# One PSUM bank moved from scores to transposes, with the value products and the first queries in another order

## The chip, the cores and the metric

The kernel runs on one core of a Trainium2 chip. The metric is the device time of one execution in microseconds, as the median of three timed runs; it is 1917.79 us for the kernel before. Everything is float32. Five engines matter: TensorE (PE, with its weight loads as PEld), VectorE (DVE), ScalarE (ACT), GpSimd (POOL) and the DMA queues issued from SyncE (SP) and from the other engines. The engines run side by side, each through its own instructions in order, and wait for each other through semaphores.

## The reference

The reference is one transformer layer on `x` of 16 batches x 512 tokens x 128 features: attention with relative positions, then a mixture of 16 experts of which each token takes one.

```python
# attention: 16 heads of 8; rel_k, rel_v have 2M + 1 = 257 rows
q, k, v = proj(Wq, bq), proj(Wk, bk), proj(Wv, bv)        # of layernorm(x)
idx = clip(r[None, :] - r[:, None], -M, M) + M            # M = 128
content  = einsum('bhqd,bhkd->bhqk', q, k)
relative = einsum('bhqd,qkd->bhqk', q, rel_k[idx])
w = softmax((content + relative) / sqrt(8))
out = einsum('bhqk,bhkd->bhqd', w, v) + einsum('bhqk,qkd->bhqd', w, rel_v[idx])
x = x + layernorm(out @ Wo.T + bo)
# experts: top 1 of 16 by x2 @ w_router.T, plus a shared one; x2 = layernorm(x)
x = x + layernorm(shared(x2) + expert(sigmoid(logit) * x2))
```

## The kernel before

The kernel has two stages. The attention stage runs over 256 passes, `i` = 0 to 255 (and 24 more in which the last results drain). A pass is one batch `b`, one of four pieces `c` of 32 queries in each 128 tokens, and one of four 128-token blocks `n`, so `k = i % 16` counts the passes of a batch (`c = k // 4`, `n = k % 4`). It handles 32 queries against all 512 keys for 16 heads. The heads go in four groups `g` of four, in the order 0, 2, 1, 3 (`ORDER`); a group's four heads and 32 queries are the 128 rows of a tile of scores, 128 x 512, which fills one bank of PSUM. The expert stage then takes sorted rows of 128 tokens at a time through the experts; the change doesn't touch it.

In the steady state pass `i` does, on PE:

- `scores`: four products `ps<-km,qb` (content) and four times eight 32-row products `ps<-relk,qr` (relative), one bank for each group. The relative products of groups 0 and 2 come first, then those of 1 and 3, over the keys within 128 of a query, which are 160 to 288 columns wide, depending on `c` and `n`.
- `turn`: the exponentials `w` of the pass before (`last = i - 1`), four tiles, each with four 128 x 128 transposes into one bank `pt`.
- `attend`: the value products of the pass five back (`old = i - 5`), `pa<-wT,v` and then `pa<-wT,relv`. In passes with `n` = 1, `join_places` puts eight small products in between for the piece nine passes back.
- at the end of many passes one extra product (`spare`): turned sums at `n` = 0, the output projection at `n` = 1, and at `k` = 6, 7, 14 and 15 the next batch's turned x, queries, keys and values.

DVE takes the row maximum of each score bank (`peak`, written `nmax`), ACT the exponentials with their sums (`exps`). The turned tiles leave PSUM through DVE (`ORDER[0]` and `ORDER[2]`, that is groups 0 and 1) and ACT (groups 2 and 3) as `wT`. DVE scales the value products by the sums (`od`, `oz`) and adds over heads (`oT`).

All these instructions are kept in the order in which the program writes them (class `InOrder`). The order of one pass is written out in the loop at lines 787 to 876. It interleaves: scores; two tiles turned; two peaks with their exponentials; copies of those two tiles; two more peaks and exponentials; value products and what leaves from them; two more tiles turned; the extra product; copies of those two tiles.

PSUM has eight banks: five for scores (`ps_s`), two for transposes (`ps_t`), one for all else (`ps_o`, function `bank`). A pool hands its banks out in turn, and a product into a bank waits until what it held last has been read.

Around the passes: `route` picks the expert of a batch's tokens and scatters their rows to DRAM, in small steps that the loop advances once a pass (lines 860 to 874); the last of these steps are four scatters issued by POOL. `expand` has POOL repeat a piece's queries into `qb` and `qr` for the scores. For `qr` the queries go through DRAM (`qd`, then 16 small DMAs into `qz`). `keys_mixed` and `keys_advance` keep on POOL the keys with end rows added. `load_x` issues four DMAs for a batch, on SP.

Before the loop, for batch 0: x is normalised and turned, then queries, keys and values are formed, one after the other in the one bank of `ps_o`, then POOL expands the first piece.

Of the kernel before, what the change touches and what calls it, by code (L numbers as in the profile page):

```python
# [9 lines left out]
F32 = mybir.dt.float32  # L10
I32 = mybir.dt.int32
AF = mybir.ActivationFunctionType
ALU = mybir.AluOpType
# [4 lines left out]
P = 128  # L18
# [32 lines left out]
def relative_attention_then_moe(  # L51
# [42 lines left out]
    with ExitStack() as actx:  # L94
# [2 lines left out]
        bp = actx.enter_context(tc.tile_pool(name="attn_batch", bufs=2))  # L97
        up = actx.enter_context(tc.tile_pool(name="attn_unit", bufs=2))
        sp = actx.enter_context(tc.tile_pool(name="attn_small", bufs=4))
        ps_s = actx.enter_context(tc.tile_pool(name="ps_s", bufs=5, space=PSUM))  # L100
        ps_t = actx.enter_context(tc.tile_pool(name="ps_t", bufs=2, space=PSUM))
        ps_o = actx.enter_context(tc.tile_pool(name="ps_o", bufs=1, space=PSUM))
        pe, act, dve, sp_q, pool = (InOrder(tc, e) for e in (nc.tensor, nc.scalar, nc.vector, nc.sync, nc.gpsimd))

# [7 lines left out]
                )  # L112

        load_x(0)


        wq = wp.tile([P, D], F32, name="wq")
# [26 lines left out]
        for i in range(2):  # L144
            sp_q.dma_start(
                kend[:, i : i + 1], bass.AP(rel_kT.tensor, rel_kT.offset + i * (NR - 1), [[0, H], [NR, HD], [1, 1]])
            )
        act.mul(bq_c, bq_c, qscale)
        bk_hi = wp.tile([P, 1], F32, name="bk_hi")
        relk = wp.tile([P, 504], F32, name="relk")  # L150
# [62 lines left out]
            )  # L213
        msum = wp.tile([P, HG, HD], F32, name="msum")

        batch, wts = {}, {}

        riders = []

        def bank(shape, name):  # L220
            return ps_o.tile(shape, F32, tag="o", name=name)
# [32 lines left out]
        def queries(b):  # L254


            xT = batch[b]["xT"]
            pq = bank([P, S], f"pq{b}")
            pe.matmul(
                pq.rearrange("p (c n q) -> p c n q", n=NKT, c=NC), wq,  # L260
                xT.rearrange("p (n c q) -> p c n q", n=NKT, c=NC), start=True, stop=True,
            )
            qp = bp.tile([P, TQ, S // TQ], F32, tag="qp", name=f"qp{b}")
            qz = bp.tile([P, 8, S // TQ], F32, tag="qz", name=f"qz{b}")
            batch[b].update(qp=qp, qz=qz)

            def leave():
                act.activation(
                    qp.rearrange("p q t -> p t q"), pq.rearrange("p (t q) -> p t q", q=TQ),
                    AF.Identity, bias=bq_c, scale=qscale,  # L270
                )
                qd = dp.tile([P, TQ, S // TQ], F32, tag="qd", name=f"qd{b}", bufs=2)
                sp_q.dma_start(qd, qp)
                batch[b]["qd"] = qd
                if b > 0:
                    queries_turned(b)

            return leave

        def queries_turned(b):  # L280
            qz, qd = batch[b]["qz"], batch[b]["qd"]
            for e in range(2):
                for i in range(TQ):
                    r = e * 64 + (7 - i) * HD
                    queue = act if b == 0 and i % 2 else sp_q
                    queue.dma_start(
                        qz[r : r + HD], qd[e * 64 : (e + 1) * 64, i, :].rearrange("(h d) t -> d h t", d=HD)
                    )

        def keys(b):  # L290

            pk = bank([P, S], f"pk{b}")
# [12 lines left out]

            return leave
# [47 lines left out]

            return leave

        def expand(b, c):

            bt = batch[b]
            tt = slice(c * 16, (c + 1) * 16)  # L360
            qb = up.tile([P, 16, HH, TQ], F32, tag="qb", name=f"qb{b}_{c}")
            pool.tensor_mul(
                qb,
                bt["qp"][:, :, tt].rearrange("p q t -> p t q").unsqueeze(2).to_broadcast([P, 16, HH, TQ]),
                mh4.unsqueeze(1).unsqueeze(3).to_broadcast([P, 16, HH, TQ]),
            )
            qr = up.tile([P, 16, 8, TQ], F32, tag="qr", name=f"qr{b}_{c}")
            pool.tensor_mul(
                qr,
                bt["qz"][:, :, tt].rearrange("p h t -> p t h").unsqueeze(3).to_broadcast([P, 16, 8, TQ]),  # L370
                mq.unsqueeze(1).unsqueeze(1).to_broadcast([P, 16, 8, TQ]),
            )
            batch[b, c] = (qb, qr)

        ORDER = (0, 2, 1, 3)

# [96 lines left out]
        def attend(b, c, n, done=None):  # L473


            wT = wts[b, c][0]
            v = batch[b]["v"]
            Rh = batch[b, c, "R"][0]
            if n == 0:
                batch[b, c, "oT"] = up.tile([P, NKT * 4, TQ], F32, tag="oT", name=f"oT{b}_{c}")  # L480
            oT = batch[b, c, "oT"]
            every3 = bank([P, 3, P], f"pa{b}_{c}_{n}")
            pa = every3[:, 0]
            for kt in range(NKT):
                vn = 1 if kt <= n - 2 else 2 if kt >= n + 2 else 0
                for g in range(HG):
                    r = slice(g * 32, (g + 1) * 32)
                    pe.matmul(
                        pa[r, :], v[:, vn, kt, r], wT[:, n, g, (kt - n) % NKT, :],
                        start=(kt == 0), stop=(kt == NKT - 1),  # L490
                    )
            t = slice(n * 4, n * 4 + 4)
            summed = lambda: None
            if done is not None:
                summed = join_places(every3[:, 1], *done)
            elif riders:
                summed = riders.pop()(every3[:, 1])
            near_done = attend_near(every3[:, 2], b, c, n)

            def leave():  # L500
                od = up.tile([P, 4, HH, TQ], F32, tag="od", name=f"od{b}_{c}_{n}")
                dve.tensor_mul(od, pa.rearrange("p (t h q) -> p t h q", h=HH, q=TQ), Rh[:, t])
                near_done()
                summed()
                dve.tensor_reduce(oT[:, t], od.rearrange("p t h q -> p t q h"), AX.X, ALU.add)

            return leave

        def attend_near(pn, b, c, n):

# [262 lines left out]
        dve.tensor_reduce(mz, mz4.rearrange("p g q -> p q g"), AX.X, ALU.add)  # L773
        dve.tensor_reduce(msum, mj.rearrange("p j g d -> p g d j"), AX.X, ALU.add)
        dve.tensor_add(bk_hi, bk_c, kend[:, 1:2])
        for f in (x_turn, queries, keys):
            f(0)()
        queries_turned(0)
        values(0)()
        expand(0, 0)  # L780
        for n in range(1, NKT):
            keys_mixed(0, n)
        if B > 1:
            load_x(1)
        later_loads()
        routes = {}
        for i in range(total + 24):
# [283 lines left out]
```

## Time and profile before

| | |
|---|---|
| median of 3 runs | 1917.79 us (1917.73 to 1917.93) |
| the profiled execution's own time | 1931.33 us |
| its span, first to last instruction | 1929.6 us |
| busy share of ACT | 63% |
| busy share of POOL | 51% |
| granted TensorE clock, mean | 0.988 |
| first scores begin | 23.44 us |
| scores of the last pass begin | 1650.68 us |

The times of the prediction are made on the profiled execution, which took 13.5 us longer than the median. A profile line has the start and length in us, the engine, the line of the program (nearly all stand under line 47, the helper that keeps the order), the operation, output<-inputs by the program's names, shapes, and the count of merged instructions; in brackets the idle time before it and what ended it. A group in the page's list has its count, total and mean time, and then the engine's idle time before it.

### The profile page before, as it was taken

The page shows a single profiled execution, that of the slowest core. Times are in us where ns is not written, and L with a number is a line of the kernel's source. Part 1 is how long each engine was busy: PE and PEld are TensorE (multiplying, and loading weights), DVE is VectorE, ACT ScalarE, POOL GpSimd, SP SyncE. Part 2 cuts the span into 40 slices and gives each one's busy share as a digit, 9 for nine tenths or more (in the row PEclk, how much of TensorE's full clock was granted, in tenths as well). Part 3 has the DMA queues.
Part 4 walks back from the last instruction along what each step waited for, and adds up shares of the span by engine and source line. Part 5 has one row for each costly group of instructions (what it writes and reads, how often), then busy time and mean ns, then how long its engine had stood idle before and what let it go on. Part 6 is the DMA issues. An engine that isn't in the chain of part 4 may idle for free. (4 is left out here: it accounts for less than half of the span.)

```text
span 1929.6 us, 88255 instructions
## 1 busy us (share of the span) xinstructions
PE 1863.7 (97%) x38268; PEld 1383.0 (72%) x38268; DVE 1528.7 (79%) x4009; ACT 1207.7 (63%) x3077; POOL 989.8 (51%) x1389
## 2 busy tenths in 40 slices
PE   6999999999999999999999999999999999779997
PEld 3667776776777777676767676776767776579997
DVE  4777787878788878788888888787878787757776
ACT  3666666666666666666666666666666665257775
POOL 4345455546455554546454555454645545236666
PEclk9999999999999999999999999999999999879999
DMA  2321100000000000000000000000000000066662
GB/s 77 65 35 40 17 23 5 15 14 5 24 5 24 4 24 3 25 3 25 3 24 5 24 4 16 12 13 16 5 18 5 18 3 9 9 176 180 183 182 87
DMA packets 88328, 68.64 MB, mean 36 GB/s; under 512 B 26440, under 2 KB 74341, under 8 KB 87809
## 3 DMA queue, kind: packets, MB, share of 16 engines
q1 hardware_dynamic: 81248, 53.60, 10.3%
q0 software_dynamic: 4384, 8.57, 1.4%
q8 instruction: 301, 4.93, 1.0%
q10 hardware_dynamic: 2304, 0.80, 0.2%
q14 instruction: 91, 0.74, 0.1%
HBM read 44.79 MB, written 18.75 MB: 33 GB/s over the span
## 5 line engine op out<-in xcount | busy, mean ns | idle before, releaser
L47 ACT ACTIVATE w<-ps,nmax 128x512 f32<-128x512 f32 x1024 | 699.0, 693 | 554.4 <-DVE nmax L47 554.0
L47 DVE TENSOR_REDUCE nmax<-ps 128x1 f32<-128x512 f32 x1024 | 655.1, 681 | 226.4 <-PE ps L47 225.2
L47 PE MATMUL pt<-ident,w 128*128 128x128 f32 x4096 | 562.0, 280 | 4.4 <-DVE wT L47 3.8
L47 PEld LDWEIGHTS pt<-ident,w 128*128 128x128 f32 x4096 | 439.7, 141 | 125.6 <-issue 85.7
L47 DVE COPY wT<-pt 128x512 f32<-128x512 f32 x512 | 348.3, 680 | 1.1 <-PE pt L47 0.7
L47 ACT COPY wT<-pt 128x512 f32<-128x512 f32 x512 | 300.9, 588 | 28.5 <-PE pt L47 26.5
L47 PE MATMUL ps<-km,qb 32*128 32x512 f32 x2048 | 298.4, 647 | 3.5 <-POOL qb L47 3.5
L47 PEld LDWEIGHTS ps<-relk,qr 64*32 64x32 f32 x8192 | 124.4, 106 | 227.6 <-issue 183.9
L47 PE MATMUL pa<-wT,v 128*32 128x128 f32 x8192 | 276.7, 276 | 2.5 <-DVE oz L47 1.4
L47 PE MATMUL ps<-relk,qr 64*32 64x288 f32 (+4 forms) x8192 | 275.5, 378 | 0.0
L47 PEld LDWEIGHTS pa<-wT,v 128*32 128x32 f32 x8192 | 208.1, 109 | 45.2 <-issue 36.0
L47 ACT ACTIVATION_READ_ACCUMULATOR w<-ps,nmax 128x1 f32 x1024 | 211.8, 207 | 0.0
L47 PE MATMUL pa<-wT,relv 128*32 128x48 f32 (+1 forms) x12288 | 199.3, 211 | 6.2 <-issue 5.4
L47 POOL TENSOR_TENSOR Rh<-R,mh 128x512 f32<-128x512 f32 x64 | 66.6, 1040 | 261.0 <-ACT R L47 253.8
L47 PEld LDWEIGHTS pa<-wT,relv 128*32 128x32 f32 x12288 | 186.8, 110 | 11.1 <-issue 11.1
L47 POOL TENSOR_TENSOR qr<-qz,mq 128x1024 f32<-128x1024 f32 x64 | 137.3, 2146 | 0.0
L47 PEld LDWEIGHTS ps<-km,qb 32*128 32x128 f32 x2048 | 82.4, 184 | 59.9 <-issue 32.0
L47 POOL TENSOR_SCALAR km<-kT,kend 128x32 f32<-128x32 f32 (+2 forms) x223 | 115.6, 520 | 1.7 <-PE ps L47 0.9
L47 POOL COPY km<-kT 128x32 f32<-128x32 f32 (+3 forms) x207 | 53.0, 261 | 113.8 <-ACT kT L47 113.8
L47 POOL DMA_INDIRECT out_dram<-f,to x73 | 75.9, 1039 | 46.8 <-issue 26.9
L47 DVE TENSOR_TENSOR od<-pa,Rh 128x128 f32<-128x128 f32 x256 | 72.9, 285 | 32.6 <-PE pa L47 29.7
L47 POOL COPY rb<-rt 128x512 f32<-128x512 f32 x64 | 39.2, 612 | 112.3 <-DVE rt L47 112.1
(168 smaller groups left out, 2331.0 us busy)
## 6 DMA issues: line engine op xcount, KB each, us to landing
gu<-_L_ffn_gate_up_proj_dram SPq DMA_DIRECT2D x73, 256.0 KB
dn<-in_L_ffn_down_proj_dram SPq DMA_DIRECT2D x73, 128.0 KB
rows<-zero SPq DMA_DIRECT2D x19, 266.0 KB
xc<-rows SPq DMA_DIRECT2D x8, 532.0 KB
x_sb<-in_L_attn_x_dram SPq DMA_DIRECT2D x64, 64.0 KB
qd<-qp SPq DMA_DIRECT2D x16, 256.0 KB
qz<-qd SPq DMA_DIRECT2D x248, 16.0 KB
relv<-vext SPq DMA_DIRECT2D x1, 1536.0 KB
```

The lines of the kernel that those rows point to most:

```text
L47: return lambda *a, **k: self.tc.keep_in_program_order(op(*a, **k))
```

## The change

It alters the order of a pass, the banks, the start, and where scatters stand.

The pass: the value products are issued straight behind the scores. The four peaks follow each other on DVE. All four tiles are turned in one stretch behind the value products: three, then on DVE `od`, `oz` and the copy of the first tile, then the fourth. `attend` hands out its DVE work in two parts, by `yield`. ACT copies both its tiles at the end of the pass.

```diff
-        ps_s = actx.enter_context(tc.tile_pool(name="ps_s", bufs=5, space=PSUM))
-        ps_t = actx.enter_context(tc.tile_pool(name="ps_t", bufs=2, space=PSUM))
+        ps_s = actx.enter_context(tc.tile_pool(name="ps_s", bufs=4, space=PSUM))
+        ps_t = actx.enter_context(tc.tile_pool(name="ps_t", bufs=3, space=PSUM))
...
                 dve.tensor_mul(od, pa.rearrange("p (t h q) -> p t h q", h=HH, q=TQ), Rh[:, t])
                 near_done()
+                yield
                 summed()
                 dve.tensor_reduce(oT[:, t], od.rearrange("p t h q -> p t q h"), AX.X, ALU.add)
-
-            return leave
+                yield
+
+            return leave()
...
             if live:
                 scores(b, c, n)
-            if last is not None:
-                T = {g: turn(*at(last), g) for g in ORDER[:2]}
+            leave_a = iter((None, None))
+            if old is not None:
+                leave_a = attend(*at(old), done=done)
+            elif done is not None:
+                join_places(bank([P, P], f"pj{b}"), *done)()
             if live:
-                for g in ORDER[:2]:
+                for g in ORDER:
                     peak(b, c, n, g)
                     exps(b, c, n, g)
             if last is not None:
+                T = {g: turn(*at(last), g) for g in ORDER[:3]}
+            next(leave_a)
+            if last is not None:
                 dve.tensor_copy(*T[ORDER[0]])
-                act.copy(*T[ORDER[1]])
-            if live:
-                for g in ORDER[2:]:
-                    peak(b, c, n, g)
-                    exps(b, c, n, g)
-            if old is not None:
-                attend(*at(old), done=done)()
-            elif done is not None:
-                join_places(bank([P, P], f"pj{b}"), *done)()
-            if last is not None:
-                T = {g: turn(*at(last), g) for g in ORDER[2:]}
+                T[ORDER[3]] = turn(*at(last), ORDER[3])
+            next(leave_a)
             if spare is not None:
                 leave = spare()
             if last is not None:
+                act.copy(*T[ORDER[1]])
                 dve.tensor_copy(*T[ORDER[2]])
                 act.copy(*T[ORDER[3]])
```

The start: 40 transposes of the identity run on PE while x is loaded (`warm`). A matrix `sel` is made on POOL. Batch 0's keys get a bank of `ps_s`. The first 16 of 64 query groups leave PSUM first, PE repeats them by eight products with `sel`, and DVE expands the first piece from there. The other queries go through DRAM as before, now all on SP. Values of batch 0 become the extra product of pass 2, and batch 1's x is loaded ahead of `kext` and `relk`.

```diff
+        def warm(n):
+
+            idle = ps_t.tile([P, NKT, P], F32, tag="t", name="idle")
+            for t in range(n):
+                pe.transpose(idle[:, t % NKT, :], ident, ident)
+
+        warm(40)
...
+        if B > 1:
+            load_x(1)
...
+        sel = up.tile([P, 8 * P], F32, tag="wT", name="sel")
+        nc.gpsimd.memset(sel, 0.0)
+        for h in range(8):
+            nc.gpsimd.affine_select(
+                sel[:, h * P : (h + 1) * P].rearrange("p (e j d) -> p e j d", e=2, j=TQ),
+                sel[:, h * P : (h + 1) * P].rearrange("p (e j d) -> p e j d", e=2, j=TQ),
+                [[-64, 2], [0, TQ], [-1, HD]], ALU.not_equal, 1.0, base=-h * HD, channel_multiplier=1,
+            )
...
+        def repeat_queries(rep_q):
+
+            for h in range(8):
+                pe.matmul(
+                    rep_q[h // 4][:, h % 4].rearrange("p t q -> p q t"), sel[:, h * P : (h + 1) * P],
+                    batch[0]["qp"][:, :, 0:16], start=True, stop=True,
+                )
+
+        def expand_first(rep_q):
+            qb = up.tile([P, 16, HH, TQ], F32, tag="qb", name="qb0_0")
+            qr = up.tile([P, 16, 8, TQ], F32, tag="qr", name="qr0_0")
+            batch[0, 0] = (qb, qr)
+            dve.tensor_mul(
+                qb,
+                batch[0]["qp"][:, :, 0:16].rearrange("p q t -> p t q").unsqueeze(2).to_broadcast([P, 16, HH, TQ]),
+                mh4.unsqueeze(1).unsqueeze(3).to_broadcast([P, 16, HH, TQ]),
+            )
+            for i in range(2):
+                dve.tensor_mul(
+                    qr[:, :, i * 4 : (i + 1) * 4, :].rearrange("p t h q -> p h t q"), rep_q[i],
+                    mq.unsqueeze(1).unsqueeze(1).to_broadcast([P, 4, 16, TQ]),
+                )
...
-        for f in (x_turn, queries, keys):
-            f(0)()
-        queries_turned(0)
-        values(0)()
-        expand(0, 0)
+        x_turn(0)()
+        rep_q = [ps_t.tile([P, 4, 16, TQ], F32, tag="t", name=f"rep_q{i}") for i in range(2)]
+        leave_q = queries(0)
+        leave_k = keys(0)
+        leave_q(0, 16)
+        repeat_queries(rep_q)
+        leave_k()
+        expand_first(rep_q)
+        leave_q(16, S // TQ)()
         for n in range(1, NKT):
             keys_mixed(0, n)
-        if B > 1:
-            load_x(1)
         later_loads()
...
+            if i == 2:
+                spare = lambda: values(0)
```

The scatters: for all but the last three batches the last steps of `route` are taken in passes with `n` = 0, right behind the sums' `rb` on POOL.

```diff
             if n == 0 and 0 <= i - 4 < total:
                 sums(*at(i - 4)[:2])
+                for r in sorted(routes):
+                    if r[0] < B - 3 and i - (r[0] + 1) * 16 - 6 >= 18:
+                        if next(routes[r], StopIteration) is StopIteration:
+                            del routes[r]
                 spare = lambda: sums_turn(*at(i - 4)[:2])
...
-                if r[0] < B - 2:
+                if r[0] < B - 3:
+                    turns = i - (r[0] + 1) * 16 - 6 in (0, 1, 2, 3, 4, 5, 6, 7, 12, 13, 14, 15)
+                elif r[0] < B - 2:
                     turns = i - (r[0] + 1) * 16 - 6 in (0, 1, 2, 3, 4, 5, 6, 7, 12, 13, 14, 15, 16, 17, 19, 20, 21)
```

More of the change, by code (lines that the diff above doesn't have):

```diff
@@ L265, in queries, with leave, turned @@
             batch[b].update(qp=qp, qz=qz)
-            def leave():
+            qd = dp.tile([P, TQ, S // TQ], F32, tag="qd", name=f"qd{b}", bufs=2)
+            def leave(t0=0, t1=S // TQ):
                 act.activation(
-                    qp.rearrange("p q t -> p t q"), pq.rearrange("p (t q) -> p t q", q=TQ),
+                    qp[:, :, t0:t1].rearrange("p q t -> p t q"),
+                    pq[:, t0 * TQ : t1 * TQ].rearrange("p (t q) -> p t q", q=TQ),
                     AF.Identity, bias=bq_c, scale=qscale,
                 )
-                qd = dp.tile([P, TQ, S // TQ], F32, tag="qd", name=f"qd{b}", bufs=2)
-                sp_q.dma_start(qd, qp)
-                batch[b]["qd"] = qd
+                if b == 0 and t0 == 0:
+                    return
+                sp_q.dma_start(qd[:, :, t0:t1], qp[:, :, t0:t1])
+                def turned():
+                    for e in range(2):
+                        for i in range(TQ):
+                            r = e * 64 + (7 - i) * HD
+                            sp_q.dma_start(
+                                qz[r : r + HD, :, t0:t1],
+                                qd[e * 64 : (e + 1) * 64, i, t0:t1].rearrange("(h d) t -> d h t", d=HD),
+                            )
                 if b > 0:
-                    queries_turned(b)
-            return leave
[L280 to L288, printed above, removed]
+                    turned()
+                return turned
+            return leave
         def keys(b):
-            pk = bank([P, S], f"pk{b}")
+            pk = bank([P, S], f"pk{b}") if b > 0 else ps_s.tile([P, S], F32, tag="s", name="pk0")
             pe.matmul(pk, wk, batch[b]["xT"], start=True, stop=True)
@@ L355, in values, with expand @@
             return leave
-        def expand(b, c):
+        def expand(b, c, eng=pool, parts=((0, 16),)):
             bt = batch[b]
-            tt = slice(c * 16, (c + 1) * 16)
             qb = up.tile([P, 16, HH, TQ], F32, tag="qb", name=f"qb{b}_{c}")
-            pool.tensor_mul(
+            qr = up.tile([P, 16, 8, TQ], F32, tag="qr", name=f"qr{b}_{c}")
+            batch[b, c] = (qb, qr)
+            for t0, t1 in parts:
+                n, tt = t1 - t0, slice(c * 16 + t0, c * 16 + t1)
+                eng.tensor_mul(
+                    qb[:, t0:t1],
+                    bt["qp"][:, :, tt].rearrange("p q t -> p t q").unsqueeze(2).to_broadcast([P, n, HH, TQ]),
+                    mh4.unsqueeze(1).unsqueeze(3).to_broadcast([P, n, HH, TQ]),
+                )
+                eng.tensor_mul(
+                    qr[:, t0:t1],
+                    bt["qz"][:, :, tt].rearrange("p h t -> p t h").unsqueeze(3).to_broadcast([P, n, 8, TQ]),
+                    mq.unsqueeze(1).unsqueeze(1).to_broadcast([P, n, 8, TQ]),
+                )
@@ new lines, in repeat_queries @@
+        def repeat_queries(rep_q):
[3 more added lines that the diff above has]
+                    batch[0]["qp"][:, :, 0:16], start=True, stop=True,
+                )
+        def expand_first(rep_q):
[3 more added lines that the diff above has]
+            dve.tensor_mul(
@@ L363, in expand @@
                 qb,
-                bt["qp"][:, :, tt].rearrange("p q t -> p t q").unsqueeze(2).to_broadcast([P, 16, HH, TQ]),
+                batch[0]["qp"][:, :, 0:16].rearrange("p q t -> p t q").unsqueeze(2).to_broadcast([P, 16, HH, TQ]),
                 mh4.unsqueeze(1).unsqueeze(3).to_broadcast([P, 16, HH, TQ]),
             )
[L367 to L372, printed above, removed]
@@ L373, in expand @@
-            batch[b, c] = (qb, qr)
+            for i in range(2):
+                dve.tensor_mul(
+                    qr[:, :, i * 4 : (i + 1) * 4, :].rearrange("p t h q -> p h t q"), rep_q[i],
+                    mq.unsqueeze(1).unsqueeze(1).to_broadcast([P, 4, 16, TQ]),
+                )
         ORDER = (0, 2, 1, 3)
```

## The prediction

> **What bounds the kernel now.** I read the page's busy shares first, then the timeline of one plain pass, then the places where TensorE does wait, then the start. The chain of waits is no help: it holds only the last microsecond. The page:
>
> ```profile
> PE 1863.7 (97%) x38268; PEld 1383.0 (72%) x38268; DVE 1528.7 (79%) x4009; ACT 1207.7 (63%) x3077; POOL 989.8 (51%) x1389
> ...
> L47 POOL TENSOR_TENSOR Rh<-R,mh 128x512 f32<-128x512 f32 x64 | 66.6, 1040 | 261.0 <-ACT R L47 253.8
> ```
>
> PE is busy 97% of the span. DVE at 79% looks like spare room, but shares don't say where in a pass it lies. POOL idles 253.8 us ahead of `Rh`. Now the timeline of a plain pass (batch 0, k = 10; start, length, engine, operation, output<-inputs):
>
> ```profile
> 84.25 1.14 PE L47 MATMUL ps<-km,qb 32*128 32x512 f32 x8
> ...
> 85.32 1.20 PE L47 MATMUL ps<-relk,qr 64*32 64x288 f32 x32
> ...
> 86.20 1.29 DVE L47 TENSOR_REDUCE nmax<-ps 128x1 f32<-128x512 f32 x2 [1.00 <-PE ps L47]
> ...
> 86.45 1.09 PE L47 MATMUL pt<-ident,w 128*128 128x128 f32 x8
> ...
> 87.40 0.68 DVE L47 COPY wT<-pt 128x512 f32<-128x512 f32 x1
> ...
> 87.48 1.08 PE L47 MATMUL pa<-wT,v 128*32 128x128 f32 x32
> ...
> 88.00 1.28 DVE L47 TENSOR_REDUCE nmax<-ps 128x1 f32<-128x512 f32 x2
> ...
> 88.38 0.75 PE L47 MATMUL pa<-wT,relv 128*32 128x64 f32 x48
> ...
> 89.05 1.09 PE L47 MATMUL pt<-ident,w 128*128 128x128 f32 x8
> ...
> 89.89 0.29 DVE L47 TENSOR_TENSOR od<-pa,Rh 128x128 f32<-128x128 f32 x1 [0.61 <-PE pt L47]
> ...
> 90.08 1.14 PE L47 MATMUL ps<-km,qb 32*128 32x512 f32 x8
> 90.10 0.28 DVE L47 TENSOR_TENSOR oz<-pa,Rz 128x128 f32<-128x128 f32 x1
> ...
> 90.30 0.37 DVE L47 TENSOR_REDUCE oT<-od 128x32 f32<-128x128 f32 x1
> 90.58 0.68 DVE L47 COPY wT<-pt 128x512 f32<-128x512 f32 x1
> ```
>
> A pass runs from one `ps<-km` to the next: 84.25 to 90.08, 5.83 us, with no hole on PE. Its six PE stretches are 1.07 (km), 1.13 (relk), 1.02 (two tiles turned), 0.90 (v), 0.68 (relv) and 1.02 (two tiles turned). DVE's first peak comes 1.95 after the pass begins, because it needs the first half of the relk products; then DVE work follows at 0.60 a step (86.20, 87.40, 88.00), so the copies hide in PE's time. Transposes alone show what happens when they don't hide (batch 0's third pass, no value products to cover):
>
> ```profile
> 39.87 0.68 DVE L47 COPY wT<-pt 128x512 f32<-128x512 f32 x1
> ...
> 40.61 0.42 PEld L47 LDWEIGHTS pt<-ident,w 128*128 128x128 f32 x4 [0.83 <-DVE wT L47]
> ```
>
> The copy ends at 39.87 + 0.68 = 40.55, and the tile waiting for that bank starts at 40.61: 0.06 after it. The start:
>
> ```profile
> 7.53 1.08 POOL L47 TENSOR_TENSOR lx_rs<-lx_ve,mhalf 128x4 f32<-128x4 f32 x1 [1.77 <-DVE lx_ve L47]
> ...
> 9.04 1.24 PE L47 MATMUL ptx<-ident,xn 128*128 128x128 f32 x4 [9.04 <-DVE xn L47]
> ...
> 23.34 2.12 POOL L47 TENSOR_TENSOR qr<-qz,mq 128x1024 f32<-128x1024 f32 x1
> ...
> 23.44 1.24 PE L47 MATMUL ps<-km,qb 32*128 32x512 f32 x4 [3.54 <-POOL qb L47]
> ```
>
> The first scores wait until 23.44 for POOL's `qb`. In the timeline the sixth pass (i = 5) starts at 52.78.
>
> **The gain: one switch.** The timeline, instruction by instruction, has transposes 0.109 apart. From the last transpose to the first of v it is 0.203, and the first transpose of a stretch is 0.055 slow. One stretch of four tiles is 1.02 + 8 x 0.109 = 1.90 where two take 2.05. So 0.15 a pass, and a plain pass would be 5.67, if nothing waited. I take it that relk straight into v drains as relk into transposes does, since every switch in this trace starts 0.07 before the modelled end of what ran before.
>
> **The price: a wait.** The fourth tile's bank is the first tile's. In the built program its first transpose waits for DVE's copy of that tile, and DVE now does, in order: four peaks, `od`, `oz`, then that copy. From the pass's start, plain wide pass:
> - first peak 1.95 (86.20 - 84.25)
> - four peaks until `od` is issued, 4 x 0.60 = 2.40
> - `od` and `oz`, 0.21 + 0.20 (89.89, 90.10, 90.30) = 0.41: the copy starts at 4.76
> - copy 0.68 and 0.06 to PE: the fourth tile starts at 5.50
> - its four transposes to the last start, 0.055 + 3 x 0.109 = 0.38, and the drain to the next pass 0.20: 6.08
>
> PE would be ready for that tile at 1.07 + 1.13 + 0.90 + 0.68 + (0.055 + 12 x 0.109) = 5.14. It waits 0.36, and the pass takes 6.08 against 5.83. Queued behind that wait are the pass's extra product and the next scores, hence the next peaks: a closed loop, and no later slack gives it back. Every pass then lasts F + 4.13, F being the first peak's start. F by the width of relk (160, 192, 224, 256, 288 columns) is 1.66, 1.72, 1.77, 1.82, 1.88, each the last less 0.053, half the width's PE time; 0.07 more where n is 2 or 3, since peaks there wait on two semaphores (1.88 in the pass at 77.40, 1.95 in the one at 84.25). Narrow passes lose more: PE gets through relk faster, DVE through four peaks no faster.
>
> An extra product behind the fourth tile costs what it does now (rows' spacing): turned sums or x 0.44, output 0.52, queries 0.88, keys 0.86, values 0.97, route's 0.28 to 0.44. In passes with n = 1 `join_places` (0.22 on PE) now falls into the wait: 6.53 against 6.67. Per pass of a batch, k = 0 to 15, before (starts of km in the timeline; these repeat from batch to batch within some hundredths):
> 6.13 6.67 6.22 5.71 6.10 6.67 6.26 6.49 6.05 7.12 6.43 6.17 6.16 6.67 6.69 6.42, sum 101.96
> after, F + 4.13 + the extra (k = 9 with its 0.45 hole inside the relv products kept):
> 6.23 6.53 6.47 6.02 6.28 6.53 6.51 6.85 6.34 6.98 6.51 6.20 6.39 6.53 6.94 6.83, sum 104.14
> So +2.18 a batch: 14 x 2.18 = 30.5, about 1.5 for batch 0 from its sixth pass (the same lists, k = 5 to 15) and 2 taken for the last batch, whose route differs: +34 us.
>
> **The start.** Removed from the chain: the values' product and its sums, POOL's `qb` and `qr`, and the round trip of queries through DRAM for the first scores. Added: eight products with `sel` (16 PE instructions at 0.109 = 1.75), three DVE products (0.60 to 0.69), and on POOL, ahead of `lx_rs`, a memset of 1024 columns (0.20 for 128, 0.11 for 16: 0.9) and eight selects (0.26 to 0.43, 0.40 taken: 3.2). POOL's setup ended at 5.76, so `lx_rs` moves from 7.53 to about 9.9, and the first transpose from 9.04 to 11.4. Then turn and copy x 1.3, queries 1.1, the first 128 columns out 0.6, pk 0.4 still ahead of them, `sel` products 1.75: scores at 16.5. Pass 1 has no spare bank and begins when the first exponential frees one (1.66 + 0.79 + 0.69 on: 19.7); its banks come 0.67 apart, so its relk starts at 22.75, its first peak at 23.5, its copy 2.40 later, and it ends 0.74 + 0.38 + 0.20 after that, at 27.2 (36.72 before). Passes 2 to 4, F + 3.72 without `od` and `oz`, with values and sums turned as extras, take 6.64, 5.61 and 5.88 and end at 45.3 (52.78 before): -7.5 us. If PE runs at half pace, as it did until 36.2 (transposes 0.213 apart), some 4 us of PE work there doubles: -3.5. If selects are as short as the shortest, -9.5. I take -7.5, since 40 transposes at 0.213 fill 8.5 us before.
>
> Trainium skill, "TensorE: Matmul & The Clock Gate", Part 1: the clock rises after one busy window of about 3.4 us and falls after an idle one. Here the granted clock fell to 0.50 for 97.6 to 101.0 after a window in which PE was busy for 1.46 of 3.40 us, so a whole idle window was not needed. By the page the 1 to 3 us between the last warming transpose and the first real one would cost nothing (-7.5); by the row it may (-3.5).
>
> **Moved at no cost.** The scatters (64 on the page of DMA issues, 1.07 on POOL in the timeline) go behind `rb` in passes with n = 0. The cover is POOL's wait for `R`, 253.8 / 62 = 4.1 us each; without it `od` is late by 1.07, and with it PE. x for batch 1 goes ahead of `kext` on SP: four issues, 1.74 to 2.99 in all, move `kext` from 7.72 to about 8.2 and `relk` by as much, and it is needed at 17.5. Now all 16 `qz` go on SP (5.50 at 77.05), ahead of `vext` and `relv`: `relv` is issued some 4 us later than 26.52, and is needed behind 45. Four score banks instead of five: the last exponential ends at F + 0.79 + 4 x 0.67 = 5.42, the next scores come at 6.08. Cover 0.66; gone, it would add one for one.
>
> Trainium skill, "TensorEngine Tiling (Array Packing)", PSUM Bottleneck: packing speeds up the products, not the copies out of PSUM, which can become the bound. It speaks against this change; the rows say how much, the page doesn't.
>
> **Sum.** +34 - 7.5 = +26.5 on the profiled execution's 1931.33 us (span 1929.6), so 1957.8; on the median of 1917.79, 1944.
>
> **Rivals.**
> - The copy is early enough and only the switch counts: -251 x 0.15 - 7.5 = -45, 1872. For it: the PE rows alone. Against: DVE would have to be at the copy 0.36 sooner in wide passes, 0.58 in narrow ones, and five instructions stand ahead of it, back to back. It pays from a wait under 0.10. 6%.
> - Peaks come late. In the pass after k = 3 the first peak stood at 2.00 instead of 1.72, after k = 9 at 2.24 instead of 1.95, behind route's small DVE operations; before, that cost nothing. In the loop it costs its full size: 3 or 4 passes of 0.3, 1 a batch, +16, 1960. Against: passes grow by 0.1 to 0.4, which lets DVE catch up. 15%.
> - The start gives nothing (POOL's selects, slow PE): 1951. 12%.
> - The wait is there but about 0.11 smaller per pass all through, and start and loop cancel: 1918. Nothing in the rows halves it. 4%.
> - The wait as worked out: 1944, 63%.
>
> For the range I go from 1930 (each pass 0.05 shorter, 12 us) to 1962 (late peaks); outside lie the first rival, the fourth, and a little above. A measurement here can tell about 0.2% from no change. Faster 7%, same 3%, slower 90%.
>
> **What would show it.** In the changed kernel's plain pass: no hole from relk to the third tile; a hole of 0.3 to 0.6 ahead of the fourth, released by DVE `wT`; km to km about 6.08; passes with n = 1 shorter, at 6.53; DVE's peaks four in a row; first scores near 16.5. I am wrong if transposes run sixteen in a row without a hole, or if the waits on PE name ACT's exponentials.

## The result and the profile after

The changed kernel takes 1949.88 us (median of 4 runs, 1947.97 to 1952.67), beside 1917.76 (1917.53 to 1917.93) for the kernel before: ratio 1.0168, 95% interval 1.0156 to 1.0180, so 32 us slower. The forecast was 1944, with a range from 1930 to 1962.

First the page of after: busy shares, then the groups that matter (count, total and mean time, then the engine's idle time before the group and what ended it).

```profile
PE 1843.9 (95%) x38324; PEld 1383.0 (71%) x38324; DVE 1517.3 (78%) x4012; ACT 1217.9 (63%) x3078; POOL 990.0 (51%) x1396
...
L47 PE MATMUL pt<-ident,w 128*128 128x128 f32 x4096 | 554.8, 280 | 57.0 <-DVE wT L47 53.8
L47 PEld LDWEIGHTS pt<-ident,w 128*128 128x128 f32 x4096 | 438.8, 141 | 130.7 <-DVE wT L47 103.0
...
L47 PE MATMUL ps<-km,qb 32*128 32x512 f32 x2048 | 294.8, 641 | 1.5 <-ACT w L47 1.5
...
L47 POOL TENSOR_TENSOR Rh<-R,mh 128x512 f32<-128x512 f32 x64 | 66.3, 1035 | 227.8 <-ACT R L47 221.7
```

TensorE's share fell from 97% to 95% although it does 56 instructions more: it now waits. The transposes have 57.0 us of idle time in front of them, ended by DVE `wT`. The scores wait 1.5 us for exponentials, so four score banks don't bind here. POOL still idles over 220 us ahead of `Rh`. The table of waits (engine and tile, what it waited for: us in total, times, longest) puts the same wait at 53.8 us for TensorE's products and at 103.0 for their weight loads:

```profile
PEld pt L47 <- DVE wT L47: 103.0, 194, 2.6
...
PE pt L47 <- DVE wT L47: 53.8, 164, 2.4
```

Neither is the loss itself, since matmul ends are modelled and overlap the hole; its size comes from starts. The plain pass, batch 0, k = 10, as before (start, length, engine, operation):

```profile
79.20 1.14 PE L47 MATMUL ps<-km,qb 32*128 32x512 f32 x8
...
80.28 1.20 PE L47 MATMUL ps<-relk,qr 64*32 64x288 f32 x32
...
81.15 2.49 DVE L47 TENSOR_REDUCE nmax<-ps 128x1 f32<-128x512 f32 x4 [1.00 <-PE ps L47]
...
81.41 1.08 PE L47 MATMUL pa<-wT,v 128*32 128x128 f32 x32
...
82.30 0.75 PE L47 MATMUL pa<-wT,relv 128*32 128x64 f32 x48
...
82.98 1.53 PE L47 MATMUL pt<-ident,w 128*128 128x128 f32 x12
...
83.55 0.28 DVE L47 TENSOR_TENSOR od<-pa,Rh 128x128 f32<-128x128 f32 x1
83.75 0.28 DVE L47 TENSOR_TENSOR oz<-pa,Rz 128x128 f32<-128x128 f32 x1
...
83.95 0.68 DVE L47 COPY wT<-pt 128x512 f32<-128x512 f32 x1
...
84.69 0.66 PE L47 MATMUL pt<-ident,w 128*128 128x128 f32 x4 [0.17 <-DVE wT L47]
...
85.27 1.14 PE L47 MATMUL ps<-km,qb 32*128 32x512 f32 x8
```

Read it against the prediction's steps. The pass begins at 79.20. The first peak stands at 81.15, 1.95 later; four peaks run in a row as one group of 2.49. Then `od` 83.55, `oz` 83.75, and only at 83.95 the copy of the first tile, 4.75 behind the pass's start (4.76 forecast). The first three tiles run from 82.98 as 12 transposes. The other four start at 84.69, 0.06 behind the copy's end (84.63); without the wait they would follow 0.109 behind the twelfth, at 84.35, so the hole is 0.34. The next pass begins at 85.27: 6.07 us (6.08 forecast) against 5.83.

The start:

```profile
1.71 7.17 PE L47 MATMUL idle<-ident 128*128 128x128 f32 x40 [1.71 <-POOL ident masks.py:199]
...
4.26 2.89 POOL L230 TENSOR_SCALAR_AFFINE_SELECT sel<-sel 128x128 f32<-128x128 f32 x8
...
9.45 1.05 POOL L47 TENSOR_TENSOR lx_rs<-lx_ve,mhalf 128x4 f32<-128x4 f32 x1
...
10.94 1.10 PE L47 MATMUL ptx<-ident,xn 128*128 128x128 f32 x4 [2.06 <-DVE xn L47]
...
16.45 1.14 PE L47 MATMUL ps<-km,qb 32*128 32x512 f32 x8
```

The warming transposes end at 8.88, the selector's eight selects take 0.36 each (0.40 forecast), `lx_rs` stands at 9.45 (9.9 forecast) and the first scores at 16.45 (16.5 forecast, 23.44 before).

The length of a pass, from one `ps<-km` to the next, by k (median over batches). "Before" is the forecast's list, from the first profile; "again" is the kernel before profiled once more (before_again, see below); "copy" is copy_first and "n1" the second run of copy_first_n1 (copy_first_n1_b), two of the experiments:

```
k              0    1    2    3    4    5    6    7    8    9   10   11   12   13   14   15   sum
before       6.13 6.67 6.22 5.71 6.10 6.67 6.26 6.49 6.05 7.12 6.43 6.17 6.16 6.67 6.69 6.42 101.96
again        6.13 6.67 6.22 5.71 6.11 6.67 6.26 6.49 6.05 6.67 6.43 5.90 6.15 6.67 6.68 6.42 101.23
forecast     6.23 6.53 6.47 6.02 6.28 6.53 6.51 6.85 6.34 6.98 6.51 6.20 6.39 6.53 6.94 6.83 104.14
after        6.22 6.47 6.46 6.01 6.27 6.47 6.51 7.17 6.33 6.47 6.80 6.01 6.38 6.47 6.86 6.75 103.65
copy         6.13 6.67 6.20 6.03 6.03 6.67 6.24 6.45 6.05 6.67 6.42 5.96 6.15 6.67 6.67 6.35 101.36
n1           6.13 6.47 6.20 6.03 6.03 6.53 6.24 6.45 6.05 6.47 6.42 5.97 6.16 6.47 6.67 6.35 100.64
```

### The profile page after: what moved, and what is told of

It is laid out like the page before. It is cut to its first block, busy times and chain, and to the rows that moved or that the text cites. A ratio compares the mean times of both kernels' runs of the same rounds, so it can differ in the third digit from the quotient of the medians.

```text
span 1946.1 us, 88498 instructions
## 1 busy us (share of the span) xinstructions
PE 1843.9 (95%) x38324; PEld 1383.0 (71%) x38324; DVE 1517.3 (78%) x4012; ACT 1217.9 (63%) x3078; POOL 990.0 (51%) x1396
## 5 line engine op out<-in xcount | busy, mean ns | idle before, releaser
L47 ACT ACTIVATE w<-ps,nmax 128x512 f32<-128x512 f32 x1024 | 689.7, 686 | 534.9 <-DVE nmax L47 534.8
L47 DVE TENSOR_REDUCE nmax<-ps 128x1 f32<-128x512 f32 x1024 | 635.9, 684 | 274.4 <-PE ps L47 271.7
L47 PE MATMUL pt<-ident,w 128*128 128x128 f32 x4096 | 554.8, 280 | 57.0 <-DVE wT L47 53.8
L47 PEld LDWEIGHTS pt<-ident,w 128*128 128x128 f32 x4096 | 438.8, 141 | 130.7 <-DVE wT L47 103.0
L47 ACT ACTIVATION_READ_ACCUMULATOR w<-ps,nmax 128x1 f32 x1024 | 207.3, 202 | 0.0
L47 PE MATMUL pa<-wT,relv 128*32 128x48 f32 (+1 forms) x12288 | 192.0, 211 | 0.0
L47 POOL DMA_INDIRECT out_dram<-f,to x73 | 75.9, 1039 | 46.8 <-issue 27.5
L47 DVE TENSOR_REDUCE oT<-od 128x32 f32<-128x128 f32 x256 | 95.3, 372 | 0.0
```

The source lines that it names most:

```text
L47: return lambda *a, **k: self.tc.keep_in_program_order(op(*a, **k))
```

## The experiments

Ratios are to the kernel before, run beside each. It stood at 1919.45 us beside order_only, reduce_ahead, copy_first and start_only; at 1921.54 beside before_again, scatter_only, banks_only and two_orders; at 1935.05 beside copy_first_n1 and copy_first_sel; and at 1920.10 beside copy_first_n1_b and n1_old_scatters. So times are compared within a set, and across sets by ratios.

**The new order alone** (`order_only`): before, with the pass's new order and banks; the start and the scatters as they were.

```diff
-ps_s bufs=5, ps_t bufs=2
+ps_s bufs=4, ps_t bufs=3
...
+the loop of a pass and attend()'s two yields, as in the change
```

> Before with the new order of a pass and its banks alone; the start and the scatters as they were. If the fourth tile's wait is the whole cost: the loop's +34 us by the prediction (1952), +38 us by the times (after is 32 above before, and the start's gain is 5.7 in the traces), so 1950 to 1958. If the moved scatters or the start bring part of the loss: clearly less, 1920 to 1945. Plain wide pass 6.07 us in both cases.

Measured: 1960.03 us, ratio 1.0208 (1.0194 to 1.0223), +40.6. The plain pass is 6.07, and weight loads wait 102.2 us for DVE `wT` (103.0 in after). The pass lengths are those of after but for two: pass 7 takes 6.82 (7.17 in after) and pass 9, in which a scatter stands here, 6.65 (6.47). So the loss lies in the order. That it is 2 us above the range has a plain place: passes 11 and 12 of batch 0 took 11.0 and 10.3 us, in after 7.4 and 6.4. These two differ by some us from run to run in every kernel here.

**The dose, upwards** (`reduce_ahead`): after, with the sum into `oT` (and `oj`) also put ahead of the copy.

```diff
             next(leave_a)
+            next(leave_a)
             if last is not None:
                 dve.tensor_copy(*T[ORDER[0]])
                 T[ORDER[3]] = turn(*at(last), ORDER[3])
-            next(leave_a)
```

> After, with VectorE's sum into oT, and in passes with n = 1 the copy oj, moved ahead of the copy of the first turned tile: the opposite of the run before. If the wait sets the pass: +0.28 us in each of 256 passes and +0.2 in 64, so +84 us, 2030 (2015 to 2045). If it doesn't: 1945 to 1955.

Measured: 2040.66 us, ratio 1.0630 (1.0614 to 1.0645). Against after's ratio this is 0.0462 x 1919.45 = +89 us. The plain pass takes 6.35, after's 6.07 plus 0.28; passes with n = 1, where the copy `oj` comes on top, take 7.01, plus 0.54. TensorE's idle time ahead of the transposes, in the page's group:

```profile
L47 PE MATMUL pt<-ident,w 128*128 128x128 f32 x4096 | 561.0, 280 | 141.8 <-DVE wT L47 101.6
```

DVE's instructions ahead of that copy thus cost one for one: the 0.28 of the sum on DVE became 0.28 or 0.29 on 11 of the 16 kinds of pass. Pass 11 grew by 0.51; why is open.

**The dose, downwards** (`copy_first`): after, with the copy ahead of `od` and `oz`.

```diff
-            next(leave_a)
             if last is not None:
                 dve.tensor_copy(*T[ORDER[0]])
                 T[ORDER[3]] = turn(*at(last), ORDER[3])
             next(leave_a)
+            next(leave_a)
```

> After, with VectorE's copy of the first turned tile moved ahead of od and oz (0.21 + 0.20 us). If the fourth tile waits for that copy: the plain wide pass falls from 6.07 to 5.67 (TensorE's own path and the wait are then about equal, F + 3.72 = 5.67), narrow ones by 0.41, sum 256 x 0.39 = 100 us, so 1850 us, below both kernels. If the loss came from four score banks or from the exponentials, nothing changes: 1945 to 1952. If another wait stands right behind this one (late peaks, the output bank that od and oz now free later): 1870 to 1930.

Measured: 1916.47 us, ratio 0.9980 (0.9971 to 0.9989). The sign is right and the loss is gone, but only some 36 us of the 100 came (0.0188 x 1919.45, from the two ratios), as the third case had it. The plain pass shows the first reason:

```profile
81.06 1.14 PE L47 MATMUL ps<-km,qb 32*128 32x512 f32 x8
...
83.01 2.48 DVE L47 TENSOR_REDUCE nmax<-ps 128x1 f32<-128x512 f32 x4 [1.00 <-PE ps L47]
...
84.84 2.09 PE L47 MATMUL pt<-ident,w 128*128 128x128 f32 x16
...
85.53 0.69 DVE L47 COPY wT<-pt 128x512 f32<-128x512 f32 x1
...
86.14 0.28 DVE L47 TENSOR_TENSOR od<-pa,Rh 128x128 f32<-128x128 f32 x1
...
86.34 0.28 DVE L47 TENSOR_TENSOR oz<-pa,Rz 128x128 f32<-128x128 f32 x1
...
86.86 0.31 PEld L47 LDWEIGHTS ps<-km,qb 32*128 32x128 f32 x8 [0.17 <-issue]
```

The four tiles now run as one group of 16. The copy starts at 85.53, not behind the fourth peak at 85.41 (81.06 + 1.95 + 2.40): it now waits for its own tile, whose last transpose ends at 85.49. It ends at 86.22, the fourth tile starts 0.06 later, and the free slot would have been 0.07 sooner. With the slow first transpose behind a hole (0.055) the pass takes 5.80, not 5.67. The second reason stands in the passes with n = 1, where `od`, `oz` and the copy `oj` now end later and the output's product waits for them:

```profile
PEld py L47 <- DVE oj L47: 11.4, 63, 0.7
```

(us in total, times: 0.18 each.) These passes take 6.67, in after 6.47. The output bank, freed by `od`, `oz` and `oj`, is the next thing to end last. And pass 3 gains nothing (6.03): its first peak is late, 2.20 behind the pass's start, behind route's DVE work. Pass 0 gains 0.09 only: its turned sums wait for POOL's `rb` (4.9 us, 15 times).

**copy_first without its new wait** (`copy_first_n1`, and once more as `copy_first_n1_b`):

```diff
+            if done is not None:
+                next(leave_a)
             if last is not None:
                 dve.tensor_copy(*T[ORDER[0]])
                 T[ORDER[3]] = turn(*at(last), ORDER[3])
+            if done is None:
+                next(leave_a)
             next(leave_a)
```

> copy_first, except in passes that join places (n = 1): there od and oz stay ahead of the copy, as in after. If those passes are long in copy_first (6.67 us, in after 6.47) because the output's product waits for the bank that od, oz and oj free: 62 x 0.2 = 12 us less than copy_first, 1904 to 1907 beside a before of 1920; all other passes as in copy_first. If the time is paid back in the passes behind them: 1917.

Measured: 1931.00 us, beside 1935.05 of before; ratio 0.9980 (0.9971 to 0.9988), no better than copy_first. The passes with n = 1 did fall to 6.47, none behind them paid it back, but those with k = 4, 8 and 12 had grown to 6.95, 6.50 and 6.61. The timeline of one with k = 4, batch 3:

```profile
348.94 0.52 PEld L47 LDWEIGHTS pa<-wT,relv 128*32 128x32 f32 x31
349.05 0.94 PE L47 MATMUL pa<-wT,relv 128*32 128x64 f32 x36
349.12 1.12 POOL L47 DMA_INDIRECT rows<-pay,at_i  x1 [0.17 <-issue]
...
349.68 0.17 PEld L47 LDWEIGHTS pa<-wT,relv 128*32 128x32 f32 x5 [0.23 <-issue]
...
350.40 0.26 PEld L47 LDWEIGHTS pa<-wT,relv 128*32 128x32 f32 x12 [0.56 <-issue]
350.42 0.38 PE L47 MATMUL pa<-wT,relv 128*32 128x48 f32 x12 [0.44 <-issue]
...
350.73 2.09 PE L47 MATMUL pt<-ident,w 128*128 128x128 f32 x16
```

A scatter starts on POOL at 349.12. Behind it TensorE's weight loads run dry twice, for 0.23 and 0.56, in the middle of the relv products, waiting for nothing that the profile shows ("issue"). The same kernel was therefore run once more.

> copy_first_n1 once more, unchanged. Its first run had holes inside the value products of passes k = 4, 8 and 12, 1.3 to 1.5 us behind each scatter's start (0.91 + 0.45 + 0.45 us in 13 batches, 23 us), and the kernel before stood at 1935 beside it, where it was at 1920 in other runs. If the holes come with the chip: where before is at 1920, those passes are at 6.03, 6.05 and 6.15 and the time at 1904 to 1908; where before is at 1935, as in the first run, ratio 0.998. If they belong to this kernel: holes and a ratio of 0.998 beside a before of 1920 too.

Measured, on the same chip in another set of runs: 1904.76 us beside 1920.10; ratio 0.9920 (0.9906 to 0.9933), and k = 4, 8 and 12 at 6.03, 6.05 and 6.16. The holes come and go with the set of runs; neither the kernel nor the chip decides. This kernel is 15 us faster than before in this set and 4 us in the first; by the ratios of this set and of the result it is some 48 us faster than after.

**Its scatters back in their old place** (`n1_old_scatters`): the scatters' part of the change undone.

```diff
-                for r in sorted(routes):
-                    if r[0] < B - 3 and i - (r[0] + 1) * 16 - 6 >= 18:
...
-                    turns = i - (r[0] + 1) * 16 - 6 in (0, 1, 2, 3, 4, 5, 6, 7, 12, 13, 14, 15)
```

> copy_first_n1 with the scatters where they were in before (passes k = 6, 8, 9 and 11). If the holes follow the scatters: none at k = 4, 8 and 12; on a chip that shows holes they stand at k = 9 and 11 as in before's first profile (0.45 + 0.28 us) and the ratio is 0.990 to 0.993; on one that shows none the time is that of copy_first_n1 within 3 us.

Measured: 1906.90 us, ratio 0.9931 (0.9917 to 0.9944), 2 us from the run beside it. Passes 4, 8 and 12 are at 6.04, 6.05 and 6.16, and pass 9, which now has a scatter, at 6.64 to 6.89 instead of 6.47: there `od` starts 0.2 late on DVE while the scatter runs on POOL (4.48 behind the pass's start instead of 4.28), and the loop passes it on. In four of these 13 batches TensorE also had a hole in pass 9, of 0.25 to 0.28 us; in pass 11, which has a scatter too, there was none. The large holes were absent in this set, so it doesn't tell which place is better when they are there.

**The kernel before once more** (`before_again`), unchanged.

> The kernel before, unchanged, profiled once more. If the 13.5 us by which its first profiled execution stood above the timed runs were holes of that one execution: a profiled time of 1916 to 1923 and passes k = 9 of 6.67 us instead of 7.12. If profiling costs this kernel 13 us each time: 1931 and 7.12 again.

Measured: 1919.92 us, k = 9 at 6.67. So most of the 13.5 us were holes of that one execution: 0.45 in pass 9 and 0.28 in pass 11 of 13 batches, 9.5 us, all gaps in TensorE's relv products, and 1.4 in passes 9 and 10 of batch 15, of the 11.4 between the two profiled executions. Its scatters stand in passes 6, 8, 9 and 11.

**The scatters alone** (`scatter_only`): before with that part of the change.

> Before with the scatters alone moved behind rb. The prediction costs them at nothing: within 3 us of before. Passes with k = 7 took 7.17 us in after from batch 3 on and 6.82 where the scatters stood as before: if the move does that by itself, +0.3 us in 13 passes, +4 us. Rival that they pay (POOL's queue freed in passes 6 to 11): -3 us.

Measured: 1921.15 us, ratio 0.9999 (0.9990 to 1.0007), k = 7 unchanged at 6.49. Nothing, as costed.

**The banks alone** (`banks_only`): before with four score banks and three for tiles.

> Before with four banks for scores and three for turned tiles, nothing else. If four score banks cost nothing, as the prediction has it (cover 0.66 us): before's time within 3 us. If the next scores wait for the last exponential: 0.1 to 0.3 us in each of 256 passes, +25 to +75 us.

Measured: 1928.91 us, ratio 1.0042 (1.0027 to 1.0056), +8. Pass 4 takes 6.30 instead of 6.11 in batches 1 to 14, behind pass 3 with its late first peak (2.06), so its exponentials are late too:

```profile
PEld ps L47 <- ACT w L47: 11.8, 58, 0.6
```

That makes some 3 us. Another 4 of the 8.8 us between this trace and that of before_again lie in batch 0, some 2 of them in passes 11 and 12, which differ between runs anyway. The prediction's cover of 0.66 was worked out for the plain pass in the new order; in the old order a pass that follows late peaks has none left.

**The start alone** (`start_only`), the change's second part.

> Before with the new start alone (warming transposes, selector, first queries repeated by TensorE, values' products in pass 2). By the prediction's sum -7.5 us: 1910. By the two traces -5.7: 1912. Rival that the start gives nothing: 1918.

Measured: 1913.66 us, ratio 0.9973 (0.9963 to 0.9983), -5.2 (-3.3 to -7.1).

**The new order only where it paid** (`two_orders`): the new start, the new order in passes that join places, the old order in all others.

```diff
-the old order
+if done is not None and last is not None: the new order
+else: the old order
```

> Before with the new start, and the new order of a pass (with its banks) only in passes with n = 1 that also join places; all other passes keep the old order, the scatters too. In after those passes took 6.47 us against 6.67, all others longer or the same. If a pass stands for itself: 4 x 0.2 us less a batch than with the start alone, -13 us, so 1900. If the neighbours pay it back (later peaks in the next pass): 1913, as with the start alone.

Measured: 1913.96 us, ratio 0.9966 (0.9954 to 0.9979), no better than the start alone. The neighbours paid nothing back (k = 2, 6, 10, 14 as with the start alone), and passes 1, 5 and 13 fell by 0.2. It was eaten by other things: pass 4 at 6.30 (four score banks), pass 9 at 6.67 (`od` late beside a scatter), and first scores at 19.27 instead of 16.45. The last one led to:

**The selector built later** (`copy_first_sel`): copy_first_n1, with `sel` built behind `lx_rs`.

> copy_first_n1, with the selector built behind lx_rs on POOL instead of ahead of it. lx_rs from 9.45 to 7.6 us, first transposes from 10.94 to 9.1, so first scores near 14.6. TensorE then idles less than 0.6 us behind the warming transposes: if that idle time (1.75 to 3.21 us in the runs so far) is what let the clock fall to 0.50 in the runs with 2.19, 2.46 and 3.21 us, it stays at 1.00 until the first scores, and the kernel is 2 to 4 us below copy_first_n1. If the fall comes from something else, first scores stand at 16.2 or later in half the runs.

Measured: 1933.27 us beside 1935.05, ratio 0.9987 (0.9977 to 0.9998), 2 us above copy_first_n1 in the same set and not 2 to 4 below it, and first scores at 17.02, not 14.6. The first transposes came at 9.78, behind an idle time of 1.74 us and not of less than 0.6, since the warming transposes ended earlier as well (8.05, in copy_first_n1 9.04). The clock fell to 0.50 all the same, at 12.16, while start_only kept it behind 1.75 us. So the length of the gap is not what decides. This run had the holes of copy_first_n1's first run too (k = 4, 8 and 12 at 6.96, 6.50 and 6.61), and k = 7 at 6.78 instead of 6.45 from batch 3 on, as after has. What stays open of both stands in the last section.

## Why the prediction was right

The mechanism was the one forecast, and each of its steps is in the trace or in a run. Some of the agreement in the sizes is luck, and is named below.

- **One switch less, 0.15.** It fits where the wait is nearly gone: copy_first's plain pass without its hole and slow restart is 5.80 - 0.07 - 0.055 = 5.67, as worked out. No run had a plain pass without any wait.
- **The fourth tile waits for the first one's copy.** Confirmed three ways: 0.06 between the copy's end and the tile; +0.28 for 0.28 more ahead of it; the loss gone with the copy moved forward. That the loss lies in the order is shown by order_only. Ahead of the copy stand six of DVE's instructions, four peaks, `od` and `oz`; the first rival counts five, the sum has all six.
- **Its size.** F + 4.13 met 12 of 16 kinds of pass within 0.08 (6.07 for 6.08, n = 1 6.47 for 6.53). Between sixth pass and last the loop lost 1620.1 - 1587.3 = 32.9 us against the second profile of before; 34 was said. Two passes were short in the forecast, 7 by 0.32 and 10 by 0.29. In pass 10 that is the rival of late peaks: DVE's `pay` waits for POOL until 2.17, and the first peak stands at 2.25 instead of 1.95. Two were long: pass 9 by 0.51, 0.45 of it a hole that belonged to one execution of before and was read as part of the kernel, and pass 11 by 0.19, where route's extra product was given 0.28 and took 0.09 (1.79 + 4.13 + 0.09 = 6.01). These four errors nearly cancel, and the holes in passes 9 and 11 of the first profile stood in the list of before as well, so a batch lost 103.65 - 101.23 = 2.42 where 2.18 was said. That they cancel is luck.
- **The start.** -5.9 us in the traces (sixth pass at 47.09 against 52.99), -5.2 alone; -7.5 was said. First scores came at 16.45 for 16.5, with luck twice over: `lx_rs` was 0.45 sooner than forecast and the steps behind it 0.4 longer, and in five of the nine profiled executions with the new start they came 0.6 to 2.8 later (last section). The step that failed is pass 1. It was given 7.5 us and took 8.9 (19.76 to 28.70): TensorE's granted clock was 0.50 from 20.7 to 27.5 in it. In two_orders, where the clock stayed at 1.00 for the first 2.6 us of this pass and came back after one stretch of 3.4, it took 7.69, though in the old order. The prediction had a slow TensorE as its other bound (-3.5).
- **At no cost.** The scatters: right. Four score banks: right in after (1.5 us of idle time), wrong as a general claim (+8 in the old order).
- **The sum.** In the traces 1947.97 - 1919.92 = +28.1, of it +32.9 loop, -5.9 start and +1.1 behind the last pass; +26.5 was said. The timed runs differ by 32.1: after's profiled execution is the fastest of its four, and before's second one, in another set of runs, stands 2 us above the 1917.76 of the result.
- **The rivals.** An early copy (1872) and cancelling parts (1918) are refuted by the result. A start that gives nothing would have been 1951, 1 us from the result and so nearer than the forecast; it is start_only, with its -5.2, that refutes it. Late peaks are real but small, one or two passes of a batch.

The Trainium skill, "TensorEngine Tiling (Array Packing)", PSUM Bottleneck, gave the direction: it says that the copy out of PSUM may become the bottleneck. Here TensorE did wait for such a copy. The amount, 0.24 us in a plain pass, came only from the order of DVE's work ahead of it.

## What to carry to other kernels

Merging stretches on the busiest engine is worth the switches that it saves, here 0.15 us a pass; but a stretch that is longer than its buffers waits for the copy that frees the first one, so that copy must be early. (As many buffers as tiles would avoid the wait too; no run here tried it.) Before merging, write down everything that the freeing engine does ahead of that copy, from the event that starts it; what is added there comes back one for one in a closed loop (0.28 for 0.28). What is taken away comes back only until the next wait (0.27 of 0.41 in the plain pass). When the copy is moved forward, look at what is now late instead, here the bank behind `od` and `oz`, and choose per pass: moving the copy took the change from 1.7% slower to 0.2% faster than before, and the choice per pass to 0.8% faster where the holes of the next section were absent, 0.2% where they were there.

## What the hardware showed unexpectedly

**Holes behind scatters.** In some sets of runs TensorE's instructions ran dry inside the packed value products, beginning 0.2 to 1.0 us behind the start of a scatter and ending at most 1.4 us behind it, in every one of 13 batches; in another set, on the same chip, the same program had none. They moved with the scatters (k = 9 and 11 in before's first profile, 4, 8 and 12 with the moved scatters), and scatters that ran beside other products (k = 6 and 8 in before, 0 in copy_first_n1) had none. They cost up to 0.92 + 0.45 + 0.45 us in 13 batches, 24 us. It is not the scatter's transfers that hold TensorE up. In copy_first_n1 the scatter's first packet starts 1.65 us or more behind the scatter's start, when the hole has ended, and in 26 of its 53 holes no DMA packet of any queue is under way. The holes of the timeline above, and the stretch behind them (length, TensorE's busy time, instructions, granted clock, DMA share, GB/s):

```profile
349.40:350.45 1.05, 0.55 (x26) 1.00 0.00 0
350.80:351.20 0.40, 0.40 (x4) 1.00 0.51 170
```

What runs beside the holes is the scatter's own instruction on POOL (1.12 us from 349.12). Whether and how it holds TensorE up, and why only in some sets, stays open; no run without scatters was made.

**The clock at the start.** The trace keeps a record of TensorE's granted clock. In all 14 traces its stretches at 1.00 and at 0.50 last whole multiples of 3.41 us (3.41, 6.83, 13.65, 61.44 us and so on), so it changes only on a fixed row of such windows, which stands elsewhere in each execution. Nine profiled executions have the new start. In four (start_only, after and both runs of copy_first_n1) the clock stayed at 1.00 from the warming transposes until the first scores. In five it fell before them, at 13.58, 13.05, 12.16, 11.56 and 11.29 (reduce_ahead, copy_first, copy_first_sel, two_orders, n1_old_scatters), and came back 3.41 or 6.83 us later. It was worth up to 2.8 us of the start: first scores at 17.02 to 19.27 instead of 16.45. In all nine it fell in pass 1, at 20.7 to 25.2.

What makes it fall was not found. Neither the idle time in front of the first transposes decides (it fell behind 1.74 us and stayed behind 1.75 to 2.06), nor how long TensorE was busy in the window before, as the profile counts it. The table by stretches has the same columns as above; first start_only, where the clock stayed behind the first row and fell behind the second, then copy_first, where it fell behind the first, then copy_first_n1, where it stayed:

```profile
11.10:14.50 3.40, 2.72 (x8) 1.00 0.28 76
17.95:21.35 3.40, 3.08 (x31) 1.00 0.27 58
```

```profile
9.65:13.05 3.40, 1.44 (x5) 1.00 0.17 32
13.10:14.50 1.40, 1.40 (x3) 0.50 0.37 114
```

```profile
7.38:10.79 3.41, 1.66 (x15) 1.00 0.34 86
```

So it fell behind 3.08 us of work and stayed behind 1.66. The Trainium skill, "TensorE: Matmul & The Clock Gate", Part 1, says that these windows run freely and don't start with the kernel, which agrees; it names an idle window as what makes the clock fall, and by these rows one with 3.08 of 3.40 us of work did so too.

**Open.** In after, reduce_ahead and copy_first_sel the first peak of pass 7 comes 0.35 late in batches 3 to 14, in copy_first and copy_first_n1 it doesn't, with the same scatters. No releaser shows in the traces. It is 4 us in after, and its cause was not found.
